# Attention products cut into four column tiles, and a small product moved behind them

## The chip, the core and the metric

The kernel runs on one core of a Trainium2 chip. The metric is device time in microseconds (us): the median of three runs is compared before and after the change. One further execution was recorded by the hardware profiler; durations and starts below come from that one.

The engines are named as in the profile: PE is the matrix engine (PEld its weight loads, which are listed apart), DVE the vector engine, ACT the scalar engine, POOL the general-purpose engine, SP the engine that issues most transfers. [...]

## What is computed

16 batches; each has 100 queries of width 640 and 722 context rows of width 384, the last four of which are "tokens". In float32 throughout:

```
query = x @ Wq;  keyt = enc @ Wk;  valt = enc @ Wv      # enc: the first 718 context rows
hs    = mha(query, keyt, valt)                          # 8 heads of 80
ca_q1 = einsum('btc,th->bch', ca, Wq_ca)[:, indices, :] # ca: the 4 tokens; 100 rows picked of 384
ca_hs1 = mha(ca_q1, x, x)
ca_hs2 = mha(ca_hs1 @ Wq, ca @ Wk_ca, ca @ Wv_ca)
out = (hs + ca_hs2) @ Wout + b_out + x
```

Two products matter here. In the first attention, the exponentials of the scores (context rows by queries) are multiplied with the values V, to which a column of ones is attached, so that the 81st column of a head's result is the sum that the result is divided by. In the tokens' attention, the exponentials of the 100 x 100 scores over x are multiplied, for each head, with a 100 x 33 matrix (32 columns made from x and the tokens' keys, and again a column of ones). This second product is called the tokens' product here; its result, `z`, is what the scores of the second small attention are summed from.

## The kernel before

A loop over the 16 batches runs with the order of the instructions of every engine as written in the program (`manual_schedule`). For batch `b` the matrix engine does, in this order: the scores of batch `b` (three groups, `scores`, L620, written to PSUM tiles `s_ps`); the tokens' product of batch `b` (`softmax2`, L808, tile `z_ps`); the small product of the next batch's x with the tokens' keys (`products`, L746, `y_ps`); the transposes of the batch before (L923, `hst_ps`); the keys of batch `b + 1` and the values of batch `b` (L471 and L440, alternating); the last keys (L565); the output projection of the batch before, where rows are complete (L951, `o_ps`); for odd `b` the queries of the next two batches (L541); and last the product of the exponentials with V (L1317, `a_ps`). While keys and values run, the other engines turn the scores into exponentials: DVE takes the maximum over keys and subtracts it, ACT exponentiates. Beside that runs the tokens' chain of the next batch: POOL multiplies and adds (L781, L788), DVE takes its maximum, ACT exponentiates (L801, `second.exponentials1()`, issued just ahead of the product with V).

PSUM tiles come from three pools of two buffers each: `ps2` (pairs of banks), `psk` and `ps1`. `a_ps`, `z_ps`, `y_ps` and two of the score tiles of the second group all take `ps1` in turn, so each waits for the reader of the tile two places before it. Instructions of PE are dispatched in order by its sequencer; an instruction that waits for several semaphores has an extra waiting instruction ahead of it.

A matmul's stationary operand can be placed in a part of the array's columns: the output's first partition says which. `QC = [(0, 64), (64, S)]` and `QZ = [(0, 32), (32, 64), (64, 96), (96, S)]` are the two ways in which the 100 queries are cut: into 64 and 36 queries, on column tiles 64 wide, or into 32, 32, 32 and 4, on column tiles 32 wide. In the program the product with V has column tiles of 64, the tokens' product column tiles of 32; the scores use four row tiles (32 rows of the array, all 128 columns); all the rest named above uses the whole array. For one head and one of six blocks of keys, each piece of queries is one matmul with 81 columns of V moving. Each float32 matmul shows up in the trace as two weight loads and two matmul records.

After the product with V, for each half of the heads, DVE takes the reciprocals of the sums (L1329), scales (L1331) and adds the tokens' result of the batch (L1338). After the tokens' product it takes reciprocals (L817) and scales (L819).

## Time and profile before

| | us |
|---|---|
| median of 3 runs | 944.19 (944.06 to 944.8) |
| span of the profiled execution | 942.4 |
| PE busy | 934.5 (99% of the span) |
| DVE, POOL, ACT busy | 674.0, 623.1, 364.7 |

The profiled execution's span runs from its first to its last instruction; the runs' time is 1.8 us more than it. PE's granted clock was 1.000 of full speed throughout. A row of a group gives, after the count, the busy time of the group in us and the mean duration of one instruction in ns; matmuls overlap, so the busy time of a group is less than count times mean. After a further bar stands the idle time of the engine just before the group, with what ended it; "issue" there means that the profile shows nothing that the engine waited for. The timeline's columns are start and length of a run of equal instructions.

### The profile page before, as it was taken

The numbers are of one execution on the slowest core, as the hardware profiler recorded it, in microseconds if no ns is written. First come the engines' busy times: TensorE is split into PE (matmuls) and PEld (weight loads), VectorE is DVE, ScalarE is ACT, GpSimd is POOL, SyncE is SP. The second block draws the span as 40 slices with busy tenths as digits, with TensorE's granted clock in tenths as the row PEclk, the third lists the DMA queues.
The fourth block names the chain that finished last, engine by engine and source line by source line (L and its number), as shares of the span: only waits on it lengthen the run. The fifth ranks groups of instructions, "written<-read, shape, count | busy, mean of one in ns | idle before, by whom it ended". The sixth has DMA issues, their size and how long they took to land.

```text
span 942.4 us, 25629 instructions
## 1 busy us (share of the span) xinstructions
PE 934.5 (99%) x11215; PEld 796.2 (84%) x11215; DVE 674.0 (72%) x1084; ACT 364.7 (39%) x605; POOL 623.1 (66%) x565
## 2 busy tenths in 40 slices
PE   9999999999999999999999999999999999999998
PEld 6998979888797888989789887987989888897866
DVE  3559794977929688595955959578693886949684
ACT  1244443524334244433424334244431534334241
POOL 5857976776738757495873948657694576748514
PEclk9999999999999999999999999999999999999999
DMA  8822024040310404003050130403113030210300
GB/s 264 296 60 87 3 70 128 1 130 3 94 60 1 117 2 135 5 11 122 1 151 3 37 82 1 139 1 95 38 40 113 1 112 7 59 53 1 95 8 29
DMA packets 45367, 62.48 MB, mean 66 GB/s; under 512 B 13448, under 2 KB 37320, under 8 KB 43656
## 3 DMA queue, kind: packets, MB, share of 16 engines
q1 hardware_dynamic: 41720, 42.97, 15.2%
q0 software_dynamic: 2512, 16.72, 6.1%
q8 instruction: 88, 1.44, 0.6%
q10 hardware_dynamic: 1024, 1.15, 0.4%
q14 instruction: 23, 0.19, 0.1%
HBM read 55.26 MB, written 5.57 MB: 65 GB/s over the span
## 4 chain that ended last, share of the span: by engine, by line
PE 96%; DVE 3%; issue 0%; DMA 0%; ACT 0%; POOL 0%; ACTq 0%; DVEq 0%
PE s_ps L620 12%; PE a_ps L1317 12%; PE v_psA L440 10%; PE v_psB L440 8%; PE kT_ps L565 8%; PE k_psA L471 7%; PE q_ps L541 7%; PE o_ps L951 7%; PE k_psB L471 6%; PE v_psC L440 3%; PE k_psC L471 3%; PE y_ps L746 2%; PE v_ps L381 2%; PE v_psD L440 2%; PE v_psE L440 2%; PE k_psE L471 1%
## 5 line engine op out<-in xcount | busy, mean ns | idle before, releaser
L781 POOL TENSOR_TENSOR e<-ca,g 100x800 f32<-100x800 f32 x64 | 99.8, 1570 | 145.2 <-DVE most L1156 125.0
L870 POOL TENSOR_TENSOR hs<-vb,p 100x640 f32<-100x640 f32 x64 | 105.6, 1659 | 45.9 <-DVE p L856 32.5
L877 POOL TENSOR_TENSOR hs<-hs,hs 100x640 f32<-100x640 f32 x48 | 113.9, 2373 | 3.8
L1317 PEld LDWEIGHTS a_ps<-vs,st 120*36 120x36 f32 (+3 forms) x3072 | 109.1, 125 | 5.6 <-issue 5.5
L1317 PE MATMUL a_ps<-vs,st 120*36 120x81 f32 (+3 forms) x3072 | 111.9, 233 | 0.0
L440 PE MATMUL v_psA<-wv_sb,enc 128*120 128x320 f32 x352 | 109.5, 434 | 0.0
L506 POOL TENSOR_TENSOR enc<-enc 128x240 f32<-128x240 f32 x135 | 98.1, 736 | 16.9 <-DMA enc<-in_enct 9.8
L1144 DVE TENSOR_TENSOR st<-st,over 120x1600 f32<-120x1600 f32 x48 | 107.6, 2243 | 0.0
L637 ACT COPY st<-s_ps 120x800 f32<-120x800 f32 x64 | 49.7, 829 | 135.6 <-PE s_ps L620 135.6
L620 PE MATMUL s_ps<-qp,kT 32*120 32x100 f32 x3072 | 97.4, 263 | 0.0
L620 PEld LDWEIGHTS s_ps<-qp,kT 32*120 32x120 f32 x3072 | 94.7, 179 | 1.6 <-issue 0.2
L788 POOL TENSOR_TENSOR e<-e,e 100x800 f32<-100x800 f32 x48 | 90.4, 1884 | 3.8
L440 PE MATMUL v_psB<-wv_sb,enc 128*120 128x320 f32 x296 | 91.9, 433 | 0.0
L471 PE MATMUL k_psA<-enc,wk_sb 128*128 128x240 f32 x360 | 87.6, 366 | 0.0
L1329 DVE RECIPROCAL rs<-a_ps 100x4 f32<-100x4 f32 x32 | 5.8, 182 | 111.0 <-PE a_ps L1317 111.0
L1156 DVE TENSOR_TENSOR most<-most,st 120x800 f32<-120x800 f32 x64 | 66.2, 1034 | 24.1 <-ACT st L631 23.0
L1152 ACT ACTIVATE st<-st 120x1600 f32<-120x1600 f32 x48 | 73.9, 1539 | 22.3 <-DVE st L1144 22.2
L471 PEld LDWEIGHTS k_psA<-enc,wk_sb 128*128 128x128 f32 x360 | 68.2, 190 | 16.8 <-DVE kT L411 0.2
L440 PEld LDWEIGHTS v_psA<-wv_sb,enc 128*120 128x120 f32 x352 | 63.2, 183 | 22.6 <-issue 0.5
L471 PE MATMUL k_psB<-enc,wk_sb 128*128 128x240 f32 x300 | 73.1, 366 | 0.3 <-DVE sm L853 0.3
L440 PEld LDWEIGHTS v_psB<-wv_sb,enc 128*120 128x120 f32 x296 | 54.0, 183 | 21.9 <-DVE vs L411 0.4
L541 PE MATMUL q_ps<-xT,wq_sb 128*128 128x200 f32 x400 | 69.1, 333 | 0.0
(146 smaller groups left out, 1732.8 us busy)
## 6 DMA issues: line engine op xcount, KB each, us to landing
vb<-va_d POOLq DMA_DIRECT2D x16, 1000.0 KB, 7.4
enc<-in_enct SPq DMA_DIRECT2D x30, 240.0 KB, 3.9
enc<-in_enct SPq DMA_DIRECT2D x15, 360.0 KB, 3.6
xT<-in_xt SPq DMA_DIRECT2D x8, 500.0 KB, 4.3
rest<-in_enct SPq DMA_DIRECT2D x31, 120.0 KB, 6.6
xn<-in_x SPq DMA_DIRECT2D x11, 320.0 KB, 5.7
out<-xn SPq DMA_DIRECT2D x11, 320.0 KB, 3.2
ca<-in_cas SPq DMA_DIRECT2D x16, 156.2 KB
```

The costliest lines, as they stand in the source:

```text
L440: nc.tensor.matmul(at[0][j][:KN, : H // 2], a_form(self.enc, f)[:, j * KN : (j + 1) * KN], wv_there.get(f, wv_sb[:, W_AT[f]]), start=first ...
L471: nc.tensor.matmul(at[:, i * KT : (i + 1) * KT], wk_sb[:, W_AT[f], i], a_form(self.enc, f), start=(first and i == 0), stop=last, skip_grou ...
L506: nc.gpsimd.tensor_tensor(out, left, right, op)
L541: nc.tensor.matmul(q_ps[:, : 2 * S].rearrange("p (j s) -> p j s", j=2), wq_sb[:, c, n * P : (n + 1) * P], xT[:, :, c, :], start=(c == 0), ...
L565: nc.tensor.matmul(bank[:, i * KT : (i + 1) * KT], weights[c], a_raw(enc, u, c), start=(i == 0 and c == 0), stop=(c == CC - 1), skip_group ...
L620: nc.tensor.matmul(s_ps[r][:n, 256 * a + lo : 256 * a + hi], kT[rows, c, u, j * KN : (j + 1) * KN], rhs, start=(a == 0 and c == 0), stop=( ...
L781: first = nc.gpsimd.tensor_tensor(to, self.ca[:, t, :].unsqueeze(1).to_broadcast([S, NH, S]), g[:, :, t].unsqueeze(2).to_broadcast([S, NH, ...
L788: nc.gpsimd.tensor_tensor(e, e, to, ALU.add)
L870: first = nc.gpsimd.tensor_tensor(to, vb[:S, t, :].rearrange("p (h d) -> p h d", h=NH), p2[:, :, t].unsqueeze(2).to_broadcast([S, NH, D]), ...
L877: nc.gpsimd.tensor_tensor(sums, sums, to, ALU.add)
L1144: return nc.vector.tensor_tensor(st[i], st[i], top.over[:KN].unsqueeze(1).to_broadcast([KN, 2, ROWS]), ALU.subtract,)
L1317: nc.tensor.matmul(a_v[lo:hi, h % 4], st[i // 2][: KEYS[i], i % 2, h * S + lo : h * S + hi], block(i, h // 4)[: KEYS[i], h % 4], start=(i ...
```

## The change

The product with V uses the same cut of the queries as the tokens' product, `QZ`, so it has four matmuls where it had two. The tokens' product of batch `b + 1` is taken out of the place behind the scores of batch `b + 1` and put behind the product with V of batch `b`. This holds for the tokens' products of batches 2 to 15; those of batches 0 and 1 stay behind their scores. DVE's two operations behind the tokens' product move with it. The constant `QC` is gone.

```
-QC = [(0, 64), (64, S)]
...
-        now.softmax2()
+        if b < 2:
+            now.softmax2()
...
-                for lo, hi in QC:
+                for lo, hi in QZ:
                     nc.tensor.matmul(
                         a_v[lo:hi, h % 4],
                         st[i // 2][: KEYS[i], i % 2, h * S + lo : h * S + hi],
...
         mine.hs2 = hs2
+        if 0 < b < B - 1:
+            second.softmax2()
         last = mine
```

## The prediction

> **What bounds the kernel now.** I read the page's shares first, then its chain of work that ended last, then PE's timeline around one batch's product with V, and last the groups with shapes kept apart. From the page (busy time; shares of the chain; the queue that brings PE its instructions: packets, MB, share):

> ```profile
> PE 934.5 (99%) x11215; PEld 796.2 (84%) x11215; DVE 674.0 (72%) x1084; ACT 364.7 (39%) x605; POOL 623.1 (66%) x565
> ...
> q8 instruction: 88, 1.44, 0.6%
> ...
> PE 96%; DVE 3%; issue 0%; DMA 0%; ACT 0%; POOL 0%; ACTq 0%; DVEq 0%
> ```

> PE is busy for 99% of the span and is 96% of the chain; PE's own waits sum to some 4 us, most of them in the opening and the first batches. So only what changes PE's time, or makes PE wait, changes the end. PE's timeline (start, length), batch 2 into batch 3:

> ```profile
> 204.50 6.99 PE L1317 MATMUL a_ps<-vs,st 120*64 120x81 f32 x192
> 211.42 1.10 PE L620 MATMUL s_ps<-qp,kT 32*120 32x100 f32 x32
> ...
> 218.23 0.54 PE L620 MATMUL s_ps<-qz,kT 32*120 32x200 f32 x8
> 218.70 0.75 PE L808 MATMUL z_ps<-y,e 100*32 100x33 f32 x64
> 219.38 1.30 PE L746 MATMUL y_ps<-m,xT 128*100 128x96 f32 x10
> 220.51 0.59 PE L923 MATMUL hst_ps<-ident,hs 100*128 100x100 f32 x5
> 220.94 0.45 PE L440 MATMUL v_psA<-wv_sb,enc 128*120 128x320 f32 x1
> ```

> Everything follows without a pause; the tokens' product takes 0.68 us from its start to that of `y_ps`, the product with V 6.92. Groups, shapes apart (busy us, mean ns):

> ```profile
> L1317 PE MATMUL a_ps<-vs,st 120*64 120x81 f32 x1024 | 102.4, 234 | 0.0
> L1317 PEld LDWEIGHTS a_ps<-vs,st 120*64 120x64 f32 x1024 | 84.4, 136 | 5.6 <-issue 5.5
> L1317 PEld LDWEIGHTS a_ps<-vs,st 120*36 120x36 f32 x1024 | 79.5, 113 | 0.0
> L808 PE MATMUL z_ps<-y,e 100*32 100x33 f32 x768 | 12.0, 198 | 0.0
> L808 PEld LDWEIGHTS z_ps<-y,e 100*32 100x32 f32 x768 | 10.2, 109 | 3.9 <-issue 3.4 <-POOL enc L506 0.5
> ```

> Two things are to be seen. Shapes that differ by 48 moving columns (81 and 33) differ by 36 ns, or, from the 4-query pieces' 192 ns, by 41: about 0.82 ns a column, so 81 columns stream for 66 ns. Loads of 64 and 36 columns differ by 23 ns: again 0.82 a column. And the weight loads idle once at each entry into a group ("issue"): the array's shape changes there.

> **What sets the pace of the product with V.** Between starts, 192 records take 6.75 us: a round of two records (both column tiles, one pass) takes 70 to 71 ns. That is the 66 ns of streaming plus some 4. Each tile's next load starts 2 ns after its matmul started and ends beneath it. So the stream of 81 columns is the bound, not the number of queries in a tile; with four tiles each still streams the same 81 columns, beside the three others.

> **Four tiles, cost by steps.** 1536 matmuls (3072 records) are added. If four tiles run side by side as two do, a round stays at 70 ns. What speaks for it is the tokens' product, the same form with 33 columns: 64 records start within 0.555 us, 8.8 ns apart, a round of four in 35 ns. Its stream is 27 ns; the rest is its load, which can start only when the tile's matmul has (26 ns for 32 columns and some 6 around it: 33). With 81 columns that load lies under 66 ns. Bounds: from below the bare stream, 66 for 70, -4 ns; from above the tokens' product's excess over its stream as a ratio, 35/30 (27 and 3 ns of overhead), or 82 ns, +12. There are 95 rounds a batch and 16 batches, 1520 in all: -6 to +18 us. I take 70 ns, by the nearest row, which is the product's own. At the entry the first load has 32 columns for 64 (-26 ns), at the exit two more tiles are staggered at 7 ns (+14): 16 x -12 ns = **-0.2 us**.

> [...] The tokens' product starts its records 8.8 ns apart on average, on four column tiles. [...]

> **The move, cost by steps** (14 of the 16 batches; single records of the trace). Taken away: start of `z_ps` to start of `y_ps`, 678 ns (552 among its records, 126 to the next shape). Scores are then followed by a whole-array product; from the last score to the tokens' product it is 257 ns in all 16 batches, and between queries (200 columns too, whole array) and scores 262. So 673 to 678 ns go, I take 675. Added: from the last record of V to the first of `z_ps` no change of shape, so one round, 66 to 70 ns; its records 535 to 552; to the scores 126; less the 161 that lie there today: 566 to 587, I take 578. Net -97 ns a batch, 14 times: **-1.4 us**. It is one change of shape, about 91 ns (257 less 200 columns at 0.83).

> **What moves on the other engines, at no cost as long as it is covered.** DVE's two steps (200 and 424 ns) now come behind `hs`:

> ```profile
> 211.54 0.18 DVE L1329 RECIPROCAL rs<-a_ps 100x4 f32<-100x4 f32 x1 [1.88 <-PE a_ps L1317]
> 211.76 0.49 DVE L1331 TENSOR_TENSOR hs<-a_ps,rs 100x320 f32<-100x320 f32 x1
> 212.28 0.49 DVE L1338 TENSOR_TENSOR hs<-hs,hs 100x320 f32<-100x320 f32 x1
> ```

> They would end at about 213.5; DVE is then idle until 215.7, when ACT has copied the first scores. Who waits for them: the score tiles of the second group take the `ps1` buffers of the second `a_ps` and of `z_ps`; the first such matmul comes 2.36 us into the scores, at about 214.4. Slack 0.9 us; gone, each 0.1 us costs 1.4 us over 14 batches. In two batches the addition in `hs` lasts 0.95 instead of 0.49, which still fits. The exponentials that the moved product reads end at 204.9 in this batch, and 1.6 us into the product with V in odd ones; the buffer of the first `a_ps` is free by then too. Behind the scores all of PE's work comes 0.68 us sooner: `v_psA` 1.73 us after the last score instead of 2.41, and it waits for ACT's first copy of the scores, which ends at 1.24 (the second, which `v_psB` needs, at 1.97, against 2.81). No transfer moves on any queue, and no POOL, ACT or SP instruction changes place.

> **Sum.** -1.4 - 0.2 = -1.6 us: a span of 940.8 against the profiled 942.4; the runs lie 1.8 us above the span, so 944.2 becomes **942.6**. I take 0.2% (1.9 us) as what a measurement tells from no change; this is just inside.

> **Rivals.**
> Rival 1, slower: PE's instructions don't come fast enough. 22,430 matmul and load records came in 88 packets, 255 each. In the product with V 768 instructions would be needed in 6.75 us where it was 384: 8.8 ns each, a packet every 2.25 us. Such a rate was held only for the 128 of the tokens' product; the scores use 480 in 7.28 us, a packet per 3.9 us, without a pause. A packet's record lasts 0.9 to 1.5 us, its lead is not shown: the period that the supply can hold lies between 0.9 and 3.9 us, and it decides from about 2.3. At 2.5 us: 3 packets x 0.25 us, less some 0.3 that about 36 queued instructions cover, 0.45 x 16 = +7; at 3.3, +46. The sequencer itself passed the tokens' 128 instructions in 1.32 us between its two waiting instructions, at most 10.3 ns each; if 36 stood queued when they began, the other 92 took 0.51 us, 5.5 each. At 10.3 the product with V would take 7.9 us: +18. Against it: no "issue" wait inside any run of products. [...]
> Rival 2, slower: four streams disturb each other, each reading the same V rows. Rounds of 75 (the tokens' product's extra 5 ns) to 82 ns: +7.6 to +18, so 950 to 961. The tokens' product, with its streams busy 27 of 35 ns, speaks against any large effect.
> Rival 3, no change: the drain is not saved, because PE pauses between the two products anyway (other operands, a late semaphore). Then 678 ns go and some 670 come: 944.0.

> **Chances.** My case 0.60, of which half comes out past -1.9 us (rounds 1 ns shorter would do it, -1.5 us); rival 1 0.13, rival 2 0.13, rival 3 0.14. So faster 0.30, within 0.2% 0.44, slower 0.26. My case alone: 941.2 to 943.5. The range goes down to 941.0 (two gaps saved a batch) and up to 956, which takes in rival 2's lower half and rival 1 at 2.5 us and leaves about 1 in 10 above.

> **What would show it.** Right: 384 records of `a_ps` in 6.75 us of starts a batch, with one tile's matmuls 70 ns apart; `z_ps` 70 ns behind, scores 126 ns behind that, `y_ps` some 260 ns behind the last score; no `s_ps` wait on DVE. Wrong: pauses inside the product with V ("issue"), rounds of 75 ns or more, or score tiles waiting for the tokens' scaling.

## The result, and the profile after

The changed kernel takes **1017.31 us** (median of 6 runs, 1010.17 to 1021.38), against 944.17 us for the kernel before (943.92 to 944.8). The ratio is 1.0765, with an interval of 1.0737 to 1.0793: it is 73 us slower, where 1.6 us less had been forecast. The profiled execution has a span of 1014.2 us, 71.8 us more than before.

From the page of the kernel after, the three lines that answer to those shown of before, and then the groups of the product with V, now L1316:

```profile
PE 953.7 (94%) x14287; PEld 807.4 (80%) x14287; DVE 673.7 (66%) x1084; ACT 364.6 (36%) x605; POOL 622.0 (61%) x565
...
q8 instruction: 112, 1.84, 0.8%
...
PE 90%; issue 6%; DVE 3%; DMA 1%; ACT 0%; POOL 0%; ACTq 0%; DVEq 0%
...
L1316 PE MATMUL a_ps<-vs,st 120*32 120x81 f32 (+3 forms) x6144 | 118.9, 233 | 33.2 <-issue 33.2
L1316 PEld LDWEIGHTS a_ps<-vs,st 120*32 120x32 f32 (+3 forms) x6144 | 109.9, 104 | 41.6 <-issue 41.5
```

PE falls from 99% to 94% of the span, although its own work is still nearly all of the chain (90%, before 96%): 6% of the chain is now "issue", time in which PE waited for nothing that the profile shows. PE's waits (total us, times, longest) say where:

```profile
PE a_ps L1316 <- issue: 33.2, 31, 1.7
PE s_ps L618 <- issue: 11.9, 12, 1.7
PE z_ps L806 <- issue: 7.7, 5, 1.9
PE idle_ps L999 <- DVE idle L996: 1.1, 1, 1.1
```

Two pauses in nearly every product with V, and more behind it, in the tokens' product and in the scores; before, none of these three had a wait worth a line. PE's timeline of the same batch that the prediction showed:

```profile
211.51 4.57 PE L1316 MATMUL a_ps<-vs,st 120*32 120x81 f32 x245
216.79 2.45 PE L1316 MATMUL a_ps<-vs,st 120*32 120x81 f32 x128 [0.70 <-issue]
220.24 0.38 PE L1316 MATMUL a_ps<-vs,st 119*32 119x81 f32 x10 [1.00 <-issue]
...
220.48 0.75 PE L806 MATMUL z_ps<-y,e 100*32 100x33 f32 x59
221.16 1.10 PE L618 MATMUL s_ps<-qp,kT 32*120 32x100 f32 x32
222.08 0.54 PE L618 MATMUL s_ps<-qz,kT 32*120 32x200 f32 x8
222.44 0.56 PE L618 MATMUL s_ps<-qp,kT 32*120 32x100 f32 x13
224.34 0.77 PE L618 MATMUL s_ps<-qp,kT 32*120 32x100 f32 x18 [1.34 <-issue]
```

The number to see is **128**. The second stretch has exactly 128 matmul records, with their 128 weight loads 256 instructions: one packet of the queue that brings PE its instructions (16 KB each; that queue grew from 88 to 112 packets, and PE's 28,574 matmul and load records make 255 a packet, as before). In 14 of the 16 batches 128 records of V stand between two pauses; in the two others 119 and 126 do, with 9 of the tokens' product and 2 of the transposes to make up the 128. Within the stretches, records start 17.5 ns apart, so a round of four takes 70 ns. The groups with shapes apart agree (`a_ps` and, for comparison, `z_ps`; busy us, mean ns):

```profile
L1316 PE MATMUL a_ps<-vs,st 120*32 120x81 f32 x3072 | 109.3, 234 | 11.2 <-issue 11.2
L1316 PEld LDWEIGHTS a_ps<-vs,st 120*32 120x32 f32 x3072 | 83.7, 109 | 26.2 <-issue 26.0
L806 PE MATMUL z_ps<-y,e 100*32 100x33 f32 x768 | 13.3, 198 | 5.2 <-issue 5.2
```

A matmul record lasts 234 ns, as it did with 64 columns. So the four streams are as fast as forecast, and PE waits between them.

**The sum.** Start to start, the 48 pauses take 64.3 us, less 0.8 us of normal pace 63.5. With the forecast's own -1.5 that makes 62.0 of 71.8 us. Most of the rest lies in four stretches of 3.41 us behind runs of pauses, all of them in the scores, in which the clock is granted at 0.50 (the mean over the span is 0.993, before 1.000). One of them, with its length, each engine's busy time and count (PE, PEld, DVE, ACT, POOL), the granted clock, the DMA engines' busy share and GB/s:

```profile
713.00:716.40 3.40, 3.40 (x71) 3.40 (x67) 0.00 (x0) 0.98 (x2) 0.00 (x0) 0.50 0.00 0
```

In the four together 230 score records start; at their usual 29 ns they would have taken 6.7 us and not 13.7, so 6.9 us are lost there. That makes 68.9; the remaining 2.9 us, shorter pauses among them, are not traced here.

### The profile page after: what moved, and what is told of

It reads as the page before. It is cut to its first block, busy times and chain, and to the rows that moved or that the text cites. A ratio compares the mean times of both kernels' runs of the same rounds, so it can differ in the third digit from the quotient of the medians.

```text
span 1014.2 us, 31766 instructions
## 1 busy us (share of the span) xinstructions
PE 953.7 (94%) x14287; PEld 807.4 (80%) x14287; DVE 673.7 (66%) x1084; ACT 364.6 (36%) x605; POOL 622.0 (61%) x565
## 3 DMA queue, kind: packets, MB, share of 16 engines
q10 hardware_dynamic: 1024, 1.15, 0.3%
## 4 chain that ended last, share of the span: by engine, by line
PE 90%; issue 6%; DVE 3%; DMA 1%; ACT 0%; POOL 0%; ACTq 0%; DVEq 0%
PE s_ps L618 12%; PE a_ps L1316 12%; PE v_psA L438 9%; PE v_psB L438 8%; PE kT_ps L563 7%; PE q_ps L539 7%; PE k_psA L469 7%; PE o_ps L949 6%; PE k_psB L469 6%; PE v_psC L438 3%; PE k_psC L469 2%; PE y_ps L744 2%; PE v_psD L438 1%; PE v_psE L438 1%; PE v_ps L379 1%
## 5 line engine op out<-in xcount | busy, mean ns | idle before, releaser
L1316 PE MATMUL a_ps<-vs,st 120*32 120x81 f32 (+3 forms) x6144 | 118.9, 233 | 33.2 <-issue 33.2
L1316 PEld LDWEIGHTS a_ps<-vs,st 120*32 120x32 f32 (+3 forms) x6144 | 109.9, 104 | 41.6 <-issue 41.5
L618 PE MATMUL s_ps<-qp,kT 32*120 32x100 f32 x3072 | 114.8, 272 | 10.0 <-issue 9.9
L618 PEld LDWEIGHTS s_ps<-qp,kT 32*120 32x120 f32 x3072 | 110.2, 187 | 13.1 <-issue 12.3
```

The costliest lines, as they stand in the source:

```text
L618: nc.tensor.matmul(s_ps[r][:n, 256 * a + lo : 256 * a + hi], kT[rows, c, u, j * KN : (j + 1) * KN], rhs, start=(a == 0 and c == 0), stop=( ...
L1316: nc.tensor.matmul(a_v[lo:hi, h % 4], st[i // 2][: KEYS[i], i % 2, h * S + lo : h * S + hi], block(i, h // 4)[: KEYS[i], h % 4], start=(i ...
```

## The experiments

Three theories stood at the start. **S**: PE's instructions come one packet per some 3.5 us, called for when the one before is entered; PE pauses wherever it goes through 256 instructions faster than that. **T**: the supply is a bare rate with a store behind it, and what ran ahead does not matter. **F**: the four column tiles or their streams are slow in themselves, or the change of operands is.

**Only the cut** (the tokens' product stays behind the scores):

```
-                for lo, hi in QC:
+                for lo, hi in QZ:
```

> Edit: the product with V in four column tiles, the tokens' product left behind the scores. Theory S (supply with a lead): PE's instructions come in packets of 256; the next packet is called only when PE's sequencer enters the one before it, and is usable some 3.5 us later; a packet used up in less makes PE wait for the rest. At 8.8 ns an instruction a packet lasts 2.24 us, so 1.2 to 1.5 us of waiting per packet inside the product with V, two a batch, as in the changed kernel; the tokens' product stands before sparse work again, so part of the waiting behind V goes: 985 to 1005 us. Theory T (supply by rate alone, some 72 instructions a us, with a store of two packets): V, scores and tokens' product still take the same 1376 instructions in a row: 1010 to 1020. Theory F (the four column tiles themselves are slow, 48 ns for each of 1536 added matmuls): 1017 to 1019, no pauses needed.

Measured: 998.16 us, ratio 1.0569 [1.0553, 1.0586]. PE's waits of this kernel:

```profile
PE a_ps L1317 <- issue: 33.9, 31, 1.9
PE s_ps L620 <- issue: 3.8, 6, 1.2
...
PE z_ps L808 <- issue: 1.0, 2, 0.5
```

The cut alone costs 54 of the 73 us, within S's range and outside both others. V's own pauses are those of the changed kernel (33.9 against 33.2 us, 31 each); those in the scores and the tokens' product are not (4.8 against 19.6). The clock stays at 1.00 in this kernel.

**Only the move** (the old cut):

```
-        now.softmax2()
+        if b < 2:
+            now.softmax2()
...
+        if 0 < b < B - 1:
+            second.softmax2()
```

> Edit: the tokens' product moved behind the product with V, which keeps two column tiles of 64. No instruction is added, and as many changes of the array's shape as before (V to tokens' product takes the place of scores to y). Theory S: only a packet that holds all of the tokens' product and is filled up with V and scores is used up too fast (2.4 to 2.8 us for 3.5), 0.2 to 0.6 us in about half of 14 batches: 945 to 948. Theory T: 944. Theory F: 944.

Measured: 947.22 us, ratio 1.003 [1.0018, 1.0043]: in S's range, where T and F had expected no change. What the move takes and brings cancels; V still has another shape here than the tokens' product, so that a change of shape comes in where one goes: from the last score to `y_ps` 257 ns instead of 935, from V's start to the scores 680 ns more. Of the 3 us, 2.6 lie in the scores, which last up to 7.49 us from first to last record instead of 7.02 (0.19 us more on average). That the tokens' 128 instructions, now directly ahead of the scores, use up the lead of the next packet is the reading by S; no run tests it by itself here. The parts do not add up: +54 and +3 make +57, not +73. Some 7 of the missing 16 us are the half-clock stretches of the profiled execution, which neither part by itself shows; for the others the reading is that with the cut, the move puts the tokens' product and the scores directly behind a V that has already used up its lead.

**Twice the columns: the same instructions, half as fast.** The first is the control, the kernel before; the second the changed kernel, with the same edit.

```
-                        a_v[lo:hi, h % 4],
+                        a_v[lo:hi, h % 4 // 2 * 2 : h % 4 // 2 * 2 + 2],
...
-                        block(i, h // 4)[: KEYS[i], h % 4],
+                        block(i, h // 4)[: KEYS[i], h % 4 // 2 * 2 : h % 4 // 2 * 2 + 2],
```

> A measuring control: the kernel before, but each matmul of the product with V streams the columns of two heads (162 for 81), so that its instructions are as many and half as dense; the sums in it are wrong. All theories: 1520 rounds x 66 ns = +100 us, 1043 to 1048, product with V 13.2 us a batch.

> The changed kernel with the same doubled columns (the sums are wrong too): four tiles, 768 instructions a batch in 13.2 us, 17 ns each, a packet lasts 4.4 us. Theory S: no waiting left inside the product with V, 0 to 0.6 us around the tokens' product in some batches: -2 to +4 us against the kernel before with doubled columns, 1042 to 1051. Theory T: the same, without the waits at the tokens' product: -2. Theory F: the added matmuls keep their price, +73: 1115 to 1122.

Measured: control 1047.51 us (1047.27 to 1047.93); changed kernel with 162 columns 1050.71 us (1049.98 to 1052.02). With as many instructions as in the changed kernel, the distance to the control shrinks from 73 to 3.2 us. F, which expected it to stay, falls; S had expected -2 to +4, T -2. PE's timeline of the changed kernel with 162 columns has one row for the whole product of a batch:

```profile
218.74 13.44 PE L1316 MATMUL a_ps<-vs,st 120*32 120x162 f32 x384
```

No pause in 384 records, and rounds of 137 ns, where the control with its two tiles has 138. This pair also shows the forecast's own mechanism, with V free of pauses. In the first batch, which has no moved product, V's start to the scores takes 13,372 ns against 13,385: -13 ns, where -12 was forecast. In the others it is 13,952, or 567 more, against 678 saved behind the scores: -111 ns a batch, -1.55 us over 14, where -1.4 and -0.2 had been forecast. The scores take that back and more: they last 0.29 us longer a batch, 4.0 us over the 14.

**Four tiles for two heads of eight only** (the tokens' product in its old place):

```
-                for lo, hi in QC:
+                for lo, hi in QZ if h >= 6 else QC:
```

> Edit: four column tiles for the last two of the eight heads only, the tokens' product left behind the scores: 96 instructions a batch more instead of 384, and the dense stretch is 192 instructions long (1.7 us), less than a packet. Theory S (packets called one ahead, usable after some 3.5 us): a packet with all 192 dense ones and 64 of the neighbours lasts 2.7 to 2.8 us, 0.7 to 0.8 us short, of which the queued instructions cover up to half a us; a packet boundary inside the stretch leaves less: 0.1 to 0.6 us a batch, and one more change of the array's shape (0.09 us a batch): 947 to 955. If the loss went with the number of added matmuls as in the kernel with the cut alone (54 us for 1536): +13.5, 957 to 959.

Measured: 949.72 us (948.9 to 950.46), ratio 1.006 [1.0045, 1.0075]. A quarter of the added instructions costs 5.6 us, a tenth of 54 and not a quarter. No product with V has a pause in it; each lasts 0.13 us longer, 2.1 us in all, and the rest lies in the work behind V. That the dense instructions go by on the lead that the slower work ahead has left is the reading by S. This is S's range, and speaks against any cost in proportion to the number of matmuls.

**More lead ahead of V's followers: the queries of odd batches moved between the tokens' product and the scores** (from the changed kernel):

```
-        if b % 2 and b + 1 < B:
...
             second.softmax2()
+        if b % 2 and b + 1 < B:
+            xT, tiles = xT_at[0], queries_tiles(p + 1)
+            for n in range(HC):
+                queries(p + 1, xT, tiles, n)
```

> Edit: the changed kernel with the queries of the next two batches (8.6 us of PE, some 200 instructions) put between the tokens' product and the scores in the seven odd batches, in place of ahead of the product with V. Theory S: the waits inside the product with V stay (two a batch), those at the tokens' product and in the scores, some 2 us a batch, go in these seven: -14 us, with up to 0.5 us each back for the wait on ACT's copy of the last queries: 1001 to 1010. Theory T (a rate of 72 a us with a store of two packets): 512 stored and 530 supplied cover the 896 of V and tokens' product when sparse work lies on both sides, so nearly all waiting goes in these seven: -28 us, 985 to 992. If the added matmuls had a price of their own: 1015 to 1020.

Measured: 1024.07 us (1020.74 to 1027.85), ratio 1.0846 [1.0811, 1.0881]. All three missed: it is 7 us slower than the changed kernel where S expected it to gain. The part that S had foreseen is there: the scores behind the queries last 7.08 us again, without pauses. But from V's start to the scores the seven odd batches take 21 us more than in the changed kernel plus the queries. PE's timeline of batch 3 shows where:

```profile
271.13 2.87 PE L1312 MATMUL a_ps<-vs,st 120*32 120x81 f32 x147
274.67 2.46 PE L1312 MATMUL a_ps<-vs,st 119*32 119x81 f32 x128 [0.67 <-issue]
279.77 2.62 PE L1312 MATMUL a_ps<-vs,st 119*32 119x81 f32 x107 [2.64 <-issue]
...
284.02 10.66 PE L539 MATMUL q_ps<-xT,wq_sb 128*128 128x200 f32 x50
```

and the table of its stretches (window, its length, then each engine's busy time and count, the granted PE clock, the DMA engines' busy share, GB/s):

```profile
274.67:277.20 2.53, 2.46 (x128) 2.29 (x128) 1.29 (x3) 0.00 (x0) 2.37 (x5) 1.00 0.92 335
277.20:279.70 2.50, 0.00 (x0) 0.00 (x0) 0.30 (x1) 0.00 (x0) 2.34 (x4) 1.00 0.12 43
279.80:282.20 2.40, 2.40 (x112) 2.40 (x115) 0.00 (x0) 0.00 (x0) 1.80 (x3) 0.78 0.02 7
282.20:284.00 1.80, 1.32 (x73) 1.15 (x63) 1.17 (x3) 0.00 (x0) 0.00 (x0) 0.50 0.00 0
284.00:294.60 10.60, 10.60 (x54) 10.35 (x50) 0.63 (x2) 1.30 (x4) 0.00 (x0) 0.81 0.01 2
```

Two things happen one after the other. The DMA engines are 92% busy while PE runs the 128 records, with the next queries' input and other transfers that used to lie under the queries; the packet that PE needs starts only 2.69 us after PE entered the one before it, and the pause lasts 2.64 us instead of some 1.2. Behind the pause the clock is granted at 0.50: the queries take 10.66 us where they took 8.62 in the kernel before, at full clock. In this profile seven stretches of 3.4 to 6.8 us stand at 0.50, five of them in an odd batch, behind a pause in V (not six, as the next expectation has it), one in an even batch's scores, one at the very end.

**The transfers kept back.** That reading was put to the test on the same kernel: in odd batches SP first waits for V's last sums, then issues the tokens' values and, behind them, x, the queries' input and the tokens' scores.

```
-            second.load()
+            if b % 2 == 0:
+                second.load()
...
+            nc.sync.dma_start(out=late_d[b : b + 1], in_=hs[:1, H - 2 : H])
+            second.load(nc.sync)
```

> The kernel with the queries of odd batches between the tokens' product and the scores, and in odd batches the transfers of the tokens' values (1000 KB) and, behind them on SP's queue, of x, the next queries' input and the tokens' scores kept back until V's last sums are scaled (a transfer of 8 bytes from hs waits for them ahead of the others). In the trace of the kernel with the queries between, the packet of instructions that PE waited for began 1.0 to 1.3 us after PE entered the one before it where the DMA engines were free, and up to 2.7 us where other transfers held them for over 0.9; the seven odd batches took 22 us more from V's start to the scores than the changed kernel's plus the queries, and six of them show a stretch of 3.4 or 6.8 us at half the granted clock behind the pause. Theory D (the transfers that now lie beside V keep PE's packets waiting, and PE's clock is granted at half after a long pause): the pauses in the odd batches' V fall back to 1.2 to 2 us, the half-clock stretches of odd batches go, and the time falls by some 22 us from 1024 to 1000 to 1008. Theory L (what was lost is the lead that the slow products ahead of V gave, whatever the transfers do): the pauses stay at 2.6 to 4.6 us and the time at 1020 to 1027.

Measured: 999.22 us (998.31 to 1003.31), ratio 1.0576 [1.0559, 1.0594]; 25 us less than without this, just past the 16 to 24 that theory D expected, where L expected next to nothing. The pauses of the odd batches are 0.6 to 2.1 us now, where they went up to 4.8. The stretches of the same batch:

```profile
267.75:273.00 5.25, 5.13 (x276) 4.94 (x276) 2.27 (x4) 0.35 (x1) 4.94 (x8) 1.00 0.17 66
273.30:275.20 1.90, 1.90 (x112) 1.90 (x114) 0.00 (x0) 0.00 (x0) 1.63 (x3) 1.00 0.04 9
275.20:277.40 2.20, 0.84 (x76) 0.72 (x64) 1.17 (x3) 0.00 (x0) 0.00 (x0) 1.00 0.00 0
277.40:286.00 8.60, 8.60 (x60) 8.42 (x50) 0.63 (x2) 1.30 (x4) 0.00 (x0) 1.00 0.77 197
```

The DMA engines now work under the queries (0.77), beside V they are nearly idle (0.17 and 0.04), and the clock is at 1.00 throughout. Over the seven odd batches V's start to the scores is 20.7 us shorter. In the whole profile, three stretches at 0.50 are left instead of seven, one of them in an odd batch and one at the very end. With the transfers out of the way, S's range for the queries' move (1001 to 1010) is met but for 2 us. The run does not part the two effects, since the late packet and the halved clock go together.

None of these kernels beats the kernel before. The gain that the change can bring is the 1.55 us of the pair above; every form of it tried here costs more in pauses than that.

## Why the prediction was wrong

- **What bounds the kernel now**: right. PE had no waits worth a line, so anything that made it wait came out in full.
- **"A round stays at 70 ns"**: right, 70 ns (4 x 17.5) inside the stretches. Rival 2, streams that disturb each other, did not happen. The streaming price of about 0.82 ns a column held too: with 81 columns more a round of the pair is 67 ns longer, 0.83 a column. Records start 17.5 ns apart in V after the change and 8.8 ns apart in the tokens' product before it, both on four column tiles.
- **The entry and exit of V, -12 ns, and the move, -97 ns a batch**: right in mechanism and nearly in size: -13 ns, and -111 ns with both in it, in the pair with 162 columns, where nothing paused. Rival 3, that the drain is not saved, is refuted by the same rows.
- **The cover on DVE**: held. DVE's two steps end late in the changed kernel only because everything does, and no score waits for them. DVE's timeline of the same batch:

```profile
220.73 0.18 DVE L1328 RECIPROCAL rs<-a_ps 100x4 f32<-100x4 f32 x1 [3.79 <-PE a_ps L1316]
220.94 0.49 DVE L1330 TENSOR_TENSOR hs<-a_ps,rs 100x320 f32<-100x320 f32 x1
221.47 0.67 DVE L1337 TENSOR_TENSOR hs<-hs,hs 100x320 f32<-100x320 f32 x1
222.06 0.20 DVE L815 RECIPROCAL rz<-z_ps 100x8 f32<-100x8 f32 x1
222.29 0.42 DVE L817 TENSOR_TENSOR z<-z_ps,rz 100x256 f32<-100x256 f32 x1
```

  They end at 222.7, 1.5 us into the scores, which first need the buffers 2.4 us in. The scores' long wait at 224.34 is "issue", and DVE is idle by then.
- **The failed step** is "Four tiles, cost by steps". It put the 1536 added matmuls at nothing because "a round stays at 70 ns", and left the question whether PE's instructions arrive fast enough to rival 1, with a chance of 0.13. The rounds do stay at 70 ns; what the sum lacked is the wait for instructions between them, +54 us for the cut alone. In the changed kernel the 31 pauses in V are 0.6 to 2.0 us from start to start, median 1.28. Rival 1 put the period that the supply can hold "between 0.9 and 3.9 us"; the pauses put it at about 3.5. Put into rival 1's own sum, 3.5 us give 3 x 1.25 - 0.3 = 3.45 us a batch, +55 us in all. That the totals agree so closely is partly luck: the sum has three short packets a batch, all inside V, and the runs show two pauses in V (41 us longer in all 16 batches) and 10 us more in the scores.
- **Why the chance was wrong**: two arguments had been set against it. "No issue wait inside any run of products" compared V with stretches that stay under the limit: the scores' 3.9 us a packet is just above 3.5, and the tokens' 128 instructions are half a packet. And the lower bound of 0.9 us was the length of a packet's own record, which is not the time from its call to its use. The trace of before held a better row: among packets that follow each other within 4 us, the spacing never falls below 3.32 us (22 cases, median 3.72), although PE's fastest 256 loads and matmuls there take 2.69 us. That is a hint and no proof, since those 256 need not be one packet.
- **What the prediction did not have at all**: that the move makes the shortage longer. Cut and move together cost 16 us more than the two alone; the tokens' product (8.8 ns a record, the densest work of all) and then the scores follow a V that has paused already, and their waits rise from 4.8 to 19.6 us. Nor had it the halved clock behind a run of pauses, some 7 of these 16 us.

## What to carry to other kernels

When a change multiplies the number of an engine's instructions without multiplying its time, work out how long one packet of 256 instructions lasts in the densest stretch, and compare it with the shortest spacing of packets anywhere in the trace (here 3.32 us in the kernel before and 3.34 us in the kernel after; about 3.5 us, some 73 instructions per us, is the estimate that fits the pauses), not with the length of a packet's record. Here finer column tiles were free only where each instruction streamed long enough: 81 columns on four tiles were too few, 162 were enough inside the product, though the scores behind it still lost 4.0 us. Heavy transfers beside a stretch that lives on its instruction supply cost time here too: keeping them back brought 25 us.

## What the runs showed of the hardware beyond that

- Instruction packets started later while data transfers held the DMA engines: with these free a packet mostly started 1.05 to 1.3 us after PE had entered the one before it (some took up to 1.7), and 1.35 to 2.7 us after where they were 0.9 busy or more.
- Pauses cost more here than their length. In the changed kernel four runs of three pauses, 4.5 to 4.9 us in sum within 11 us, and in the kernel with the queries between single pauses of 3.9 to 4.8 us (in two batches runs of shorter ones) were followed, some 3 to 5.5 us after the last pause began, by stretches of 3.41 or 6.83 us at a granted clock of 0.50. No clean limit shows: a run of three pauses in the changed kernel's second batch, 4.6 us in sum, was followed by none. In the kernel before, the mean over the span was 1.000.
- A change of the array's shape cost about 0.1 us of PE's time, by the pair with 162 columns: -111 ns a batch, of which -13 are V's own.
